# Four recurrent layers on one core: the first eight steps' PSUM banks begun one step at a time, the adapters' first products one step later, x of the first block loaded in two parts

## The chip, the cores and the metric

The kernel runs on one core of a Trainium2 chip. The metric is the time of one execution on the device in microseconds (us). Beside the times there is a profile of one execution, taken by the hardware profiler: when each instruction of each engine started and ended, and what it waited for. The engines are named PE (TensorE, matmuls; PEld are its weight loads), DVE (VectorE), ACT (ScalarE), POOL (GpSimd) and SP (SyncE, which issues the DMAs here).

## The reference

x is [32, 256, 256] (batch, time, features), cond is [32, 256]. Four layers follow each other, each added to x:

```python
# layer 0: GRU over time, conditioned          (h starts at 0)
z = sigmoid(x_t W_z + h U_z + cond C_z + b_z)
r = sigmoid(x_t W_r + h U_r + cond C_r + b_r)
hh = tanh(x_t W + r * h U + cond C + b)
h = (1 - z) * h + z * hh
# layer 1: leaky recurrence over time           (h starts at cond)
gate = sigmoid(h Wh' + x_t Wz' + b)
h = tanh(h * (1 - alpha) + gate * x_t)
# layer 2: gated cumulative sums over time, with W_f, W_i, W_h
# layer 3: adapter: matrices made from cond (W1, gelu, W2), applied to x per batch row
```

`r * h U` is `(r * h) @ U`. Everything is float32. Layers 0 and 1 are recurrences over 256 steps; layer 3's matrices depend on cond alone, and the gates of layer 2 for the first six eighths of the time can be computed while the recurrences still run.

## The kernel before, in words

**Two phases.** Phase 1 (lines 180 to 772) runs the two recurrences together, step by step: step t does layer 0 for time t and layer 1 for time s = t - 1. Phase 2 (lines 777 to 953) does what is left of layer 2, and layer 3, in ten turns over eight groups of four batch rows, by an order written out by hand (`TURN`). This change touches phase 1 only.

**The order.** Both phases stand under `tc.manual_schedule()`: each engine executes its instructions in the order of the program, and waits between engines are semaphores that the framework puts in. Work beside the recurrences is kept in dictionaries by step (`transfers`, `products`, `moves`, `additions`, `sigmoids`, `sums`, line 221), filled before the loop with `at(when, t, f)`, and called at fixed places of the loop with `due(when, t)`.

**One step on TensorE** (loop at line 693). In the order of the program: the product `hT` x `U_rz` (in texts: U_rz(t)), on which r and z depend; what `products` holds for this step; in step 1 the begin of layer 1's bank; the product for layer 1 with `w_l_Wz` (l_Wz); the product `rhT` x `U_h`, on which the candidate hh depends; `h1T` x `w_l_Wh` (l_Wh); then `project(t + 1)`, the product of the next step's x with `W_rzh` (W_x). Each product is 8 matmuls (2 halves of the contraction by 4 column strips of the array, line 571), and each float32 matmul shows as 2 weight loads and 2 matmuls in the profile, 16 in all. All of these are line 573. Between U_rz and U_h, ACT computes r (L657), DVE r * h (L725) and its transpose rhT (L649). Between U_h and the next U_rz, ACT computes tanh (L657), DVE a scan that combines z, h and hh (L639) and the transpose hT (L649).

**Banks and their begin.** The sums of a step are gathered in a PSUM bank of 512 columns: r, z and hh of one step take 3 x 64 = 192 columns, so a bank holds two steps, t and t + 2 (U0 = 2), and there are two such banks at a time. `begin` (line 593) writes the terms that do not depend on time (bias and cond's products, in `v`) with four matmuls, `start=True`, for all steps of the bank at once. For t < 8 it multiplies float32 `v` by an identity; from t = 8 on bfloat16 `parts`, prepared by DVE in steps 1 to 6 (lines 380 to 388: `rest` L237, `cast` L233). `project` calls it when a bank is new: for steps 0, 1, 4, 5, 8, 9 and so on, ahead of W_x of that step and thus at the end of the step before. Layer 1 has a bank of its own, for 2 steps first and then for 8 (`begin_1`, line 671); the first one of 8 steps is begun at the end of step 2, behind W_x(3), with float32 `v` and 512 columns.

**The adapters' weights** (`ada_weights`, line 400): eight pieces of W2. Piece n has its two products (`multiply`, L429, tile `pw`, here pw(0) and pw(1)) in steps t and t + 1, its four loads of 256 KB in transfers of steps t - 5 to t - 2, its bias at t - 2, a copy by ACT at t + 2, additions by POOL at t + 2 and t + 3, its store at t + 4. The first t is 5 (line 519), each next one 4 later. The adapters' matrices (`ada_matrix`, L489 and following) come after them, each in 6 steps. Layer 2's early gate products (`gate_unit`, L93 or L115) go into the steps from 35 on that have none of these (lines 535 to 557); phase 2 reads them back from DRAM.

**Loads at the start.** SP issues them in this order: cond, condT, vecs, bias rows, C_rzh (2), W1, x of steps 0 to 7 (`load_x(0)`, 256 KB), W_rzh (768 KB), U_rz (512 KB), U_h, l1_Wz, l1_Wh, x of steps 8 to 15, base_down, base_up (256 KB each).

## Time and profile before

| What | us |
|---|---|
| median of 3 runs | 955.35 |
| lowest and highest of them | 955.17, 957.66 |
| the profiled execution: its own time | 956.46 |
| the profiled execution: span from first to last instruction | 954.6 |
| phase 1 (until the first product of phase 2) | 737.6 |
| hT of step 0 begins | 13.96 |
| mean step over the recurrence | 2.82 |
| median step | 2.80 |

The granted TensorE clock was 0.995 of full speed. A step is counted from one hT (the first of the two transposes, L649) to the next. A row of the profile's timeline gives start, length, engine, line, operation, what is written and read, shape and count; in square brackets, how long the engine was idle before it and what ended that. "issue" there means that the profile shows nothing that the engine waited for. A row of the chain of waits gives start, length and engine, line and count of the work that was on the way to the end. Lengths of matmuls are those of a pipeline and overlap: the start of the next row tells what one cost.

### The profile page before, as it was taken

What the parts mean: (1) busy time and instruction counts of PE and PEld (TensorE: products, weight loads), DVE (VectorE), ACT (ScalarE), POOL (GpSimd) and SP (SyncE); (2) the same over time, 40 slices, a digit from 0 to 9 for tenths busy, and PEclk for the clock granted to TensorE, in tenths of its full rate; (3) what the DMA queues carried; (4) which work ended last, traced back from release to release, by engine and by line L of the source; (5) the groups of instructions that cost most, each with busy time, mean ns of one, the idle gap of its engine ahead of it and who ended that gap; (6) DMA issues with size and microseconds to landing.
All of it is one profiled execution on the core that took longest, in us unless ns stands there. A gap on an engine that the chain in (4) does not pass through costs nothing.

```text
span 954.6 us, 55121 instructions
## 1 busy us (share of the span) xinstructions
PE 919.4 (96%) x22806; PEld 630.6 (66%) x22806; DVE 788.4 (83%) x3409; ACT 572.3 (60%) x2648; POOL 236.5 (25%) x594
## 2 busy tenths in 40 slices
PE   7999999999999999999999999999998989999978
PEld 4666666666666666666666666666675557777756
DVE  5767788888888888888888888888776799999994
ACT  3455555555555555555555555555554788889972
POOL 1233322222222222222222222222222022222222
PEclk9999999999999999999999999999999999999989
DMA  8344212222222222222222222432241457777543
GB/s 265 108 126 147 79 51 92 65 73 92 70 92 77 92 66 67 91 70 90 69 86 76 65 97 66 131 119 83 73 128 54 122 165 230 224 228 224 188 158 117
DMA packets 104158, 107.71 MB, mean 113 GB/s; under 512 B 9153, under 2 KB 86241, under 8 KB 103906
## 3 DMA queue, kind: packets, MB, share of 16 engines
q1 hardware_dynamic: 103906, 104.18, 34.4%
q8 instruction: 179, 2.93, 1.3%
q14 instruction: 73, 0.60, 0.2%
HBM read 59.06 MB, written 45.09 MB: 109 GB/s over the span
## 4 chain that ended last, share of the span: by engine, by line
PE 80%; DVE 13%; ACT 3%; issue 2%; DMA 1%; POOL 0%; DVEq 0%; POOLq 0%; ACTq 0%
PE p L573 45%; PE ps_l L889 10%; PE pg L93 10%; PE ps_c L93 5%; DVE h L639 5%; PE p L600 3%; PE ps_g L93 2%; PE pw L489 2%; ACT other L657 2%; DVE hT L649 1%; ACT r L657 1%; DVE rh L725 1%; DVE cc L848 1%; DVE gate_g L138 1%; PE pw L429 1%
## 5 line engine op out<-in xcount | busy, mean ns | idle before, releaser
L573 PE MATMUL p<-w_W_rzh,xT 128*32 128x192 f32 x4096 | 214.8, 326 | 0.2 <-issue 0.2
L657 ACT ACTIVATE other<-p 128x32 f32<-128x32 f32 x512 | 74.2, 199 | 172.9 <-PE p L573 172.9
L639 DVE TENSOR_TENSOR_SCAN h<-other,keep 128x64 f32<-128x64 f32 x512 | 121.3, 278 | 66.3 <-ACT other L657 62.7
L573 PE MATMUL p<-w_U_rz,hT 128*32 128x128 f32 x4080 | 165.4, 279 | 6.0 <-DVE hT L649 0.2
L750 POOL TENSOR_TENSOR pairs<-xT,hT 128x64 f32<-128x64 f32 x256 | 82.2, 321 | 326.9 <-DVE other L766 273.6
L657 ACT ACTIVATE r<-p 128x32 f32<-128x32 f32 x510 | 72.8, 195 | 149.0 <-PE p L573 149.0
L689 POOL TENSOR_TENSOR X<-pairs,h1T 128x64 f32<-128x64 f32 x256 | 103.0, 402 | 214.9 <-DVE rhT L649 211.8
L573 PEld LDWEIGHTS p<-w_U_rz,hT 128*32 128x32 f32 x4080 | 97.4, 108 | 84.3 <-DVE hT L649 83.4
L639 DVE TENSOR_TENSOR_SCAN pre<-other,pairs 128x128 f32<-128x128 f32 x256 | 123.3, 481 | 34.2 <-ACT pairs L757 0.7
L573 PEld LDWEIGHTS p<-w_W_rzh,xT 128*32 128x32 f32 x4096 | 124.9, 110 | 22.4 <-issue 1.9
L573 PEld LDWEIGHTS p<-w_l_Wz,pairs 128*32 128x32 f32 x4096 | 79.2, 110 | 86.0 <-issue 69.2
L757 ACT ACTIVATE pairs<-h1T,leak 128x32 f32<-128x32 f32 x510 | 133.6, 314 | 0.4
L573 PE MATMUL p<-w_l_Wz,pairs 128*32 128x64 f32 x4096 | 120.3, 225 | 5.1 <-ACT keep L707 1.6
L573 PE MATMUL p<-w_U_h,rhT 128*32 128x64 f32 x4080 | 106.6, 221 | 0.4 <-issue 0.4
L573 PE MATMUL p<-w_l_Wh,h1T 128*32 128x64 f32 x4080 | 104.7, 219 | 0.8 <-issue 0.7
L725 DVE TENSOR_TENSOR rh<-r,h 128x32 f32<-128x32 f32 x510 | 74.9, 188 | 32.1 <-ACT r L657 5.7
L649 DVE STREAM_TRANSPOSE hT<-h 128x32 f32<-128x32 f32 x512 | 84.1, 198 | 0.0
L882 POOL TENSOR_TENSOR X<-X,w 128x512 f32<-128x512 f32 x32 | 41.4, 1306 | 165.3 <-DVE w L875 76.8
L649 DVE STREAM_TRANSPOSE rhT<-rh 128x32 f32<-128x32 f32 x510 | 80.0, 195 | 0.0
L573 PEld LDWEIGHTS p<-w_l_Wh,h1T 128*32 128x32 f32 x4080 | 76.4, 110 | 1.3 <-issue 1.0
L573 PEld LDWEIGHTS p<-w_U_h,rhT 128*32 128x32 f32 x4080 | 69.7, 108 | 5.5 <-issue 0.6
L686 ACT ACTIVATE h1T<-pre 128x64 f32<-128x64 f32 x256 | 69.5, 271 | 1.4 <-DVE pre L639 1.4
(108 smaller groups left out, 1470.5 us busy)
## 6 DMA issues: line engine op xcount, KB each, us to landing
adapted<-wm SPq DMA_DIRECT2D x128, 128.0 KB
wt<-adapted SPq DMA_DIRECT2D x28, 512.0 KB
xT<-in_xT_dram SPq DMA_DIRECT2D x32, 256.0 KB
w<-in_W_dram SPq DMA_DIRECT2D x32, 256.0 KB
out_dram<-y SPq DMA_DIRECT2D x32, 256.0 KB
gates<-gate_i SPq DMA_DIRECT2D x48, 128.0 KB
gates<-gate_s SPq DMA_DIRECT2D x48, 128.0 KB
gates<-gate_g SPq DMA_DIRECT2D x48, 128.0 KB
```

The lines of the kernel that those rows point to most:

```text
L93: nc.tensor.matmul(ps[:, 0 : (h1 - h0) * (rows.stop - rows.start) * CT].rearrange("p (h b t) -> p h b t", h=h1 - h0, t=CT), w[:, k, e * P ...
L573: last = nc.tensor.matmul(ps[j * B : (j + 1) * B, cols], hT[:, k, :], w[:, k, j, :], start=False, stop=False, skip_group_check=True, tile_ ...
L639: nc.vector.tensor_tensor_scan(*(x[:, ns].rearrange("p n u -> p (n u)") for x in (done, other, pairs)), 0.0, ALU.mult, ALU.add,)
L649: nc.vector.transpose(dst[:, c], src[:, bass.ts(c, B)])
L657: nc.scalar.activation(dst[:, bass.ts(c, B)], src[:, bass.ts(c, B)], function)
L686: nc.scalar.activation(flat(h1T), pre, AF.Tanh)
L689: return nc.gpsimd.tensor_add(X2[:, :, :, s], by_chunk(pairs1.pop(s)[:, :, 0]), h1s.pop(s))
L725: rh_done = nc.vector.tensor_mul(rh[:, cs], r[:, cs], h[:, cs])
L750: nc.gpsimd.tensor_add(by_chunk(pairs1[t][:, :, 0]), x_of(t), hT)
L757: nc.scalar.activation(by_chunk(pairs1[s][:, :, 1])[:, c], h1T[:, c], AF.Copy, scale=leak[:, c : c + 1],)
L882: after(nc.gpsimd.tensor_add(x, x, ws[g][:, b]), on_vector)
L889: nc.tensor.matmul(ps[:, e, :], matrices[row][:, m, k, e * P : (e + 1) * P], src[:, k, :], start=(k == 0), stop=(k == NC - 1),)
```

## The change

Three edits.

1. `begin` no longer makes its bank; `bank` does. For t < 8, `project` begins the 192 columns of its own step alone, in each step; from step 8 on the two steps of a bank are begun together, as before. The begin of layer 1's banks is the same as before.
2. The first piece of the adapters' weights has t = 6 instead of 5. All pieces, the adapters' matrices and what fills the steps between them follow from that t.
3. x of steps 0 to 7 is loaded in two DMAs: steps 0 and 1 where the whole was, ahead of W_rzh; steps 2 to 7 behind U_h.

```diff
         def load_x(i):
             xTs[i] = xp.tile([P, NC, TB, B], FP, name=f"xT_{i}", tag="xT")
-            nc.sync.dma_start(out=xTs[i], in_=a["xT"][:, i])
+            if i > 0:
+                nc.sync.dma_start(out=xTs[i], in_=a["xT"][:, i])
+
+        def load_first_x(steps):
+            nc.sync.dma_start(out=xTs[0][:, :, steps], in_=a["xT"][:, 0, :, steps])
...
             load_x(0)
+            load_first_x(slice(0, 2))
             w_x = load_wq("W_rzh", 3)
             w_urz = load_wq("U_rz", 2)
             w_uh = load_wq("U_h", 1)
+            load_first_x(slice(2, TB))
             w_1z = load_wq("l1_Wz", 1)
...
-        t = 5
+        t = 6
         for n in range(NW):
             ada_weights(n, t)
             t += 4
...
-        def begin(tag, cols, steps, t):
+        def bank(tag):
+            bufs = 2 if tag == "0" else 1
+            return pa.tile([P, 512], FP, name=f"p_{tag}", tag=f"p_{tag}", bufs=bufs)
+
+        def begin(ps, u, cols, steps, t):
...
-            ps = pa.tile([P, 512], FP, name=f"p_{tag}", tag=f"p_{tag}", bufs=2 if tag == "0" else 1)
             for j in range(Q):
                 nc.tensor.matmul(
-                    ps[j * B : (j + 1) * B, 0 : steps * n].rearrange("p (u n) -> p u n", n=n),
+                    ps[j * B : (j + 1) * B, u * n : (u + steps) * n].rearrange(
+                        "p (u n) -> p u n", n=n
+                    ),
...
         def project(t):
             if t // 2 % U0 == 0:
-                ps = begin("0", slice(0, 3 * S), U0, t)
-                for u in range(U0):
-                    p_0[t + 2 * u] = ps
+                p_0[t] = p_0[t + 2] = bank("0")
+                if t >= 8:
+                    begin(p_0[t], 0, slice(0, 3 * S), U0, t)
+            if t < 8:
+
+                begin(p_0[t], t // 2 % U0, slice(0, 3 * S), 1, t)
             return product(p_0[t], cols_0(t, 0, 2), x_of(t), w_x)
 
         def begin_1(s, steps):
-            ps = begin("1", slice(3 * S, 4 * S), steps, s)
+            ps = bank("1")
+            begin(ps, 0, slice(3 * S, 4 * S), steps, s)
```

More of the change, by code (lines that the diff above doesn't have):

```diff
@@ L608, in begin @@
                 )
-            return ps
         def cols_0(t, first, last):
```

## The prediction, made before the changed kernel ran

> **What bounds the kernel now.** I read the page's head and its DMA part first, then the chain of waits of the first 16 us, then TensorE's timeline from 8 to 30 us, then the start times of the hT transposes (L649) over the whole recurrence.

> ```profile
> span 954.6 us, 55121 instructions
> ...
> PE 919.4 (96%) x22806; PEld 630.6 (66%) x22806; DVE 788.4 (83%) x3409; ACT 572.3 (60%) x2648; POOL 236.5 (25%) x594
> ...
> q8 instruction: 179, 2.93, 1.3%
> ```

> PE's 96% is not the limit. One step runs from one hT to the next, and in 237 of 255 steps that takes 2.80 us within 0.03, whatever extra products stand in the step: the recurrence is a chain PE, ACT, DVE, PE. The last line counts PE's instruction blocks: 179 packets, 2.93 MB, thus 16,384 bytes each. It matters below.

> The chain of the start:

> ```profile
> 11.38 0.46 ACT hyT L373 x2
> 11.85 1.28 ACT L374
> 13.15 0.23 ACT keep L707
> 13.38 0.18 ACT other L657 x2
> ...
> 14.20 0.69 PE p L573 x16
> ```

> Step 0 is held by ScalarE: gelu (L373), its table load (L374), then z (L707). PE is not in it.

> The rows in which the changed work stands (start, length; 16 matmuls are one product):

> ```profile
> 15.63 0.43 PE L573 MATMUL p<-w_U_h,rhT 128*32 128x64 f32 x16
> 15.88 0.41 PE L573 MATMUL p<-w_l_Wh,condT 128*32 128x64 f32 x16
> 16.10 0.83 PE L573 MATMUL p<-w_W_rzh,xT 128*32 128x192 f32 x16
> 17.05 0.64 PE L573 MATMUL p<-w_U_rz,hT 128*32 128x128 f32 x16
> ...
> 18.96 0.83 PE L573 MATMUL p<-w_W_rzh,xT 128*32 128x192 f32 x16
> 19.61 1.04 PE L600 MATMUL p<-v,ident 128*32 128x512 f32 x8
> 20.47 0.62 PE L573 MATMUL p<-w_U_rz,hT 128*32 128x128 f32 x16
> ...
> 22.35 0.85 PE L600 MATMUL p<-v,ident 128*32 128x384 f32 x8
> 22.99 0.86 PE L573 MATMUL p<-w_W_rzh,xT 128*32 128x192 f32 x16
> 23.64 0.65 PE L573 MATMUL p<-w_U_rz,hT 128*32 128x128 f32 x16
> ...
> 26.83 0.62 PE L573 MATMUL p<-w_U_rz,hT 128*32 128x128 f32 x16
> 27.27 0.38 PE L429 MATMUL pw<-w,hyT 128*32 128x256 f32 x1
> 27.91 0.42 PE L429 MATMUL pw<-w,hyT 128*32 128x256 f32 x4 [0.26 <-issue]
> ```

> From U_h to the next U_rz, PE has a window of 1.42 us (15.63 to 17.05) that h's way through ACT and DVE takes anyway. Lengths overlap, so costs are differences of starts: U_h 0.24, l_Wh 0.23, W_x 0.65 (22.99 to 23.64); together 1.11, cover 0.30. A begin of 384 columns costs 0.64 (22.35 to 22.99), of 512 columns 0.86 (19.61 to 20.47), so 192 columns cost 0.32.

> **The begins.** Before: two begins of 384 columns at steps 0 and 1 (behind ACT and hT, free) and two ahead of U_rz(4) and U_rz(5). After hT's start U_rz can begin 0.24 later (16.81, 17.05). hT(3) starts at 23.00, so U_rz(4) is 23.64 - 23.24 = 0.40 late; hT(4) at 26.27, so U_rz(5) is 26.83 - 26.51 = 0.32 late. After: 0.32 in every step.
> - Steps 0 and 1 begin less: 0. U_rz(1) waited for hT, PE idle 0.5 us before it.
> - Ahead of U_rz(2): 0.32 into a cover of 0.30: +0.02.
> - Ahead of U_rz(3): begin_1's 0.86 already overfills that window, nothing covers: +0.32.
> - Ahead of U_rz(4) and U_rz(5): 0.32 less each: -0.32, -0.32.
> - Ahead of U_rz(6) and U_rz(7): PE idle 0.22 and 0.37 there; DVE's casts (L237, L233) stretch the window: 0, at worst +0.10.

> Sum -0.30. Were 192 columns no cheaper than 384 (0.64 each), it would be 0.34 + 0.64 + 0 + 0 + 0.42 + 0.27 = +1.7 instead.

> **Products a step later.** pw(0) leaves step 5 (3.41 us from hT to hT) for step 6. Without its stop at 27.27 step 5 would take about 2.87 between U_rzs instead of 3.08: -0.21. In steps 6 and 7 pw takes 0.42 in the window after U_rz, where step 6 shows it costs nothing. SP only issues the weights' loads later; they are needed at 29.9 instead of 27.2. The chain of adapters' matrices ends at step 234 instead of 233, gate products fill to step 254 instead of 253, the last gate store goes from step 257's place to 258's. None is on the path: phase 2 starts at 737.58 on POOL's X (L689), and first fetches of gates follow it. In step 256 DVE has the room for one guard (0.55): idle 1.10 ahead of its transpose. 0, bounded by -0.1 and +0.6.

> **x in two parts.** Before, 256 KB lie ahead of W_rzh, which lands at 11.87 (SP's next issue waits for it). 192 KB less at 0.75 us per 256 KB (landings 13.25, 14.01, 14.77) bring it about 0.55 earlier, and U_rz and U_h too. Step 0's z waits for the table load until 13.15, W_x(0) ends at 12.6 already: 0. The rest of x passes l_Wz and l_Wh, which have the same bytes ahead as before but more packets: by the trace's DMA records a 2,048-byte packet takes 86 ns, 768 bytes 36, 128 bytes 13, 512 bytes 27. Old: 128 x 86 / 16 = 0.69 us. New: 256 x (20, an estimate between 13 and 27) and 256 x 36, over 16 engines: 0.90. So l_Wz lands 0.2 later, at about 15.0 instead of 14.8, for a use at 14.89 that has 0.35 us before U_h: +0.0 to +0.1. One more DMA puts base_up's issue behind W_rzh's landing (SP's ninth DMA waits for the first); behind it on SP stand x of steps 16 to 23 and the adapters' loads for step 6. None is wanted within 10 us: 0. [...]

> **What the sum hides: PE's instruction blocks.** PE stops eight times in the recurrence with "issue", no releaser: at 18.35, 27.91, 44.58, 69.73, 103.25, 708.94, 712.96, 717.53 (starts after the stop). I counted PE's instructions (load, matmul, semaphore) in the trace: every one stands 194 or 193 past a multiple of 256, a 16,384-byte block, and 1.3 to 1.5 us after the end of a q8 packet. A packet starts about 0.8 us after the boundary before it, takes 1.0, and is used 1.4 later: 3.2 of the 4.1 us that PE takes for a block. When DMA is full it starts late. The steps over 2.80 after step 7 are 11, 20, 32, 42, 57, 247, 249, 250, by 0.54, 0.57, 0.30, 0.26, 0.16, 0.67, 0.64, 0.55: 3.69 us, most of them such stops. [...]

> The change moves these boundaries: each additional begin is 16 instructions. By step 5 begins 2 and 3 add 32. The boundary that stopped PE inside pw(0) then falls after the first pair of U_rz(5), on the chain. The boundary before it is at 22.35 now, 22.39 then (l_Wh(3)), and 5.56 us passed from there to 27.91, because the next weights' loads (issued 20.1 to 22.7, as before) fill DMA. So U_rz(5), due at 26.53, would go on at 27.95. From there 1.42 and, with DVE's L237, 1.44: U_rz(6) at 30.80 instead of 29.91. The first three parts and this together give **+0.9**; without the stop -0.5. I take +0.9, the row's own delay.

> After step 8 boundaries are 64 instructions, about 1.04 us, earlier; the adapters' DMAs 2.80 later. The block after (4.15 on) meets them with 4.15 - 1.04 - 2.80 = 0.31 us in favour. Each late stop shorter by 0.31 gives -2.3 of 3.69; x, gate weights and matrices don't shift, so I take the half and less: **-1.0**. Bounds: -3.7 (all go) to +3.7 (as many again).

> Sum +0.9 - 1.0 = -0.1. In the profiled execution (956.46, span 954.6, 1.86 outside) that is 956.4; it stands 1.1 above the median of the runs, 955.35, so I put the forecast at **955.2**.

> **Rivals.**
> 1. The stop at U_rz(5) doesn't come (its packet starts earlier), and late stops shrink as worked out: -0.5 - 1.0 to -2.3, at **953.6**. For it: W_x(0) and (1) run 0.6 earlier, so the first block is asked for earlier. Against: 22.35 is hardly moved. Chance 0.2.
> 2. Slower: boundaries fall onto U_rz or U_h instead of covered places. One stop costs up to 1.4 there (U_rz(5) above), against 0.2 in pw(0). With the +0.9 and one or two more late stops than now, **957.2**; four more decide for over 958.2. For it: packets 18 and 35 are used at 1.46 and 1.54 us after their end, just at the limit. Chance 0.2.
> 3. The begins are not hidden: PE pays 0.32 in all six steps, 1.92 - 0.72 saved = +1.2, with the stop 957.5. Against: PE idles 0.30 before 17.05. Chance 0.1.

> The forecast's case (954.2 to 956.3) has 0.5. About 0.3% (2.9 us) is what a measurement of this kernel can tell from no change, and the three runs of before span 2.5. Below 952.5 only rival 1's tail, 0.06; above 958.2 tails of 2 and 3, 0.08. The range 953.0 to 957.4 leaves out about 0.2.

> **What would show it.** hT(0) at 13.96 as before; U_rz(2) at 17.07; U_rz(3) 0.3 later, at 20.8; U_rz(4) at 23.66; an "issue" stop of about 1.4 in U_rz(5) at 26.5; steps 8 and on 2.80; stops 1.3 to 1.5 us after q8 packets, 64 instructions earlier. Wrong if step 0 gets shorter, if U_rz(2) starts over 0.2 later, or if a wait other than "issue" appears after step 8.

## The result, and the profile after

Over 14 executions of each kernel the changed kernel took 959.87 us (median; 957.28 to 962.21), the one before 957.09 (955.17 to 958.94): ratio 1.0028, 95% interval 1.0018 to 1.0039. A second comparison (r1 below, 12 executions against 35) gave 961.38 against 959.72, ratio 1.0018 (1.0002 to 1.0034). The change makes the kernel slower, by 2.8 us in the first comparison and 1.7 in the second; forecast was -0.1. The 955.35 that the forecast started from was the median of three runs, 1.7 below that of 14: of the 4.7 us between 955.2 and 959.87, 1.7 lie in the starting point and 2.9 in the change (+2.8 instead of -0.1).

The profiled execution took 961.18 (granted clock 0.989 of full speed). The lines of its page that answer to those of before:

```profile
span 959.4 us, 55161 instructions
...
PE 923.6 (96%) x22826; PEld 635.1 (66%) x22826; DVE 788.4 (82%) x3409; ACT 573.5 (60%) x2648; POOL 236.6 (25%) x594
...
q8 instruction: 179, 2.93, 1.3%
```

The work is the same, and as many instruction packets: 179 of 16,384 bytes for PE's 45,875 recorded instructions (45,837 before), 256 to a packet. The start, first ScalarE's timeline, then TensorE's:

```profile
12.04 0.47 ACT L379 ACTIVATE hyT<-ph,vecs 128x32 f32<-128x32 f32 x2 [6.01 <-PE ph L371]
12.51 1.28 ACT L380 ACT_TABLE_LOAD   x1
13.80 0.23 ACT L721 ACTIVATE keep<-p 128x64 f32<-128x64 f32 x1
```

```profile
14.85 0.64 PE L579 MATMUL p<-w_U_rz,hT 128*32 128x128 f32 x16 [0.63 <-DVE hT L659]
...
15.98 0.43 PE L579 MATMUL p<-w_l_Wz,pairs 128*32 128x64 f32 x16 [0.26 <-DMA w_l_Wz<-in_l_Wz_dram]
...
17.78 0.62 PE L579 MATMUL p<-w_U_rz,hT 128*32 128x128 f32 x16
...
21.50 0.62 PE L579 MATMUL p<-w_U_rz,hT 128*32 128x128 f32 x16
...
24.35 0.62 PE L579 MATMUL p<-w_U_rz,hT 128*32 128x128 f32 x16
...
27.20 0.63 PE L579 MATMUL p<-w_U_rz,hT 128*32 128x128 f32 x16
```

All of step 0 is 0.65 later (z at 13.80 instead of 13.15). Take that off, and U_rz(2) to U_rz(5) start at 17.13, 20.85, 23.70 and 26.55, where the prediction has 17.07, 20.8, 23.66 and 26.5. The predicted stop in U_rz(5) is not in this execution.

Why step 0 is later: TensorE's rows for the same 16 matmuls, before and after.

```profile
7.19 1.48 PE L341 MATMUL pv<-w_c,condT 128*32 128x384 f32 x16
```

```profile
7.10 2.23 PE L347 MATMUL pv<-w_c,condT 128*32 128x384 f32 x16
```

They are untouched by the change. Over all traces hT(0) starts between 13.7 and 15.7 us: from 13.9 to 15.3 without any of the edits, from 13.7 to 15.2 with all of them. The 0.65 are within that spread, so I take them for chance. The clock rows show 1.00 in both, so they do not name the cause.

Three stretches add up to a profiled execution: up to hT(0), the recurrence to hT(255), and the rest. After against before: 14.61 and 13.96; 721.35 and 719.74; 223.43 and 220.91. The first eight steps took 23.72 instead of 24.24 us, as the begins and pw(0) had it; the steps after them, of 2.80 each, were late by 6.4 us in sum instead of 4.0 (here and below, what steps over 2.85 us have above 2.80); and phase 2 took 2.5 us more, of which the prediction has nothing.

**Phase 2.** The windows view (busy time of each engine, then granted clock), first of before, then of after:

```profile
737.50:741.00 3.50, 3.42 (x8) 2.80 (x9) 0.00 (x0) 0.00 (x0) 0.14 (x2) 0.51 0.66 186
768.00:772.00 4.00, 4.00 (x20) 3.49 (x19) 4.00 (x5) 3.94 (x7) 0.50 (x2) 1.00 0.92 247
```

```profile
739.00:743.00 4.00, 2.86 (x7) 2.32 (x8) 0.03 (x1) 0.26 (x1) 0.44 (x2) 0.51 0.42 123
770.00:774.00 4.00, 3.45 (x8) 2.82 (x9) 4.00 (x5) 3.95 (x5) 2.22 (x3) 0.50 0.42 121
```

Both are at half clock near 738 (and near 925, of which below); after is so again at 770, and TensorE's timeline there shows the price, 6.70 us for 16 matmuls that took 3.72:

```profile
766.83 3.72 PE L889 MATMUL ps_l<-X,wt 128*128 128x256 f32 x16 [2.85 <-POOL X L882]
```

```profile
770.55 6.70 PE L903 MATMUL ps_l<-X,wt 128*128 128x256 f32 x16 [2.85 <-POOL X L896]
```

The idle time ahead of them is the same 2.85 us. The traces' halved stretches last 3.41 or 6.83 us and start on a grid of 3.41 us: those of after, at 739.06, 769.78 and 930.21, are 9 and 47 times 3.413 apart, those of before, at 737.57 and 925.30, 55 times. On that grid PE idled for 2.08 us (61%) of the window that ended at 769.78, just before the clock fell; before, it idled for 1.95 (57%) of the one that ended at 768.29, and the clock stayed. That is no threshold: in runs told below the clock also fell behind windows with 46% (e1, 734.62 to 738.04), 50% (b2, 738.28 to 741.69) and 51% of it idle (e13, 105.20 to 108.61). So the window need not be idle as a whole; what decides besides the idle share is open.

What the second stretch costs can be read across the traces of the kernels whose idle time on PE behind the recurrence was left as it is. From hT(255) to the end it is 220.5 to 221.7 us in the six that do not have it, 223.4 to 223.7 in the four that have one of 6.83 us (after, r1, e8 and e11, the last being the kernel before with 64 instructions more), and 221.3 in e10, which has one of 3.41.

**Theories.** F: PE's instruction blocks. The change moves the boundaries and the transfers, and blocks arrive too late where they arrived in time. C: the clock; the change only shifts phase 2 on the grid, and the excess is the second halved window. B, within F: it takes a burst of transfers ahead of the packet. N: chance.

### The profile page after: what moved, and what is told of

Same layout as the page of the kernel before. It is cut to its first block, busy times and chain, and to the rows that moved or that the text cites. A ratio compares the mean times of both kernels' runs of the same rounds, so it can differ in the third digit from the quotient of the medians.

```text
span 959.4 us, 55161 instructions
## 1 busy us (share of the span) xinstructions
PE 923.6 (96%) x22826; PEld 635.1 (66%) x22826; DVE 788.4 (82%) x3409; ACT 573.5 (60%) x2648; POOL 236.6 (25%) x594
## 3 DMA queue, kind: packets, MB, share of 16 engines
q8 instruction: 179, 2.93, 1.3%
## 4 chain that ended last, share of the span: by engine, by line
PE 81%; DVE 11%; ACT 3%; issue 2%; DMA 1%; SPq 1%; POOL 0%; DVEq 0%; POOLq 0%; ACTq 0%
PE p L579 45%; PE ps_l L903 11%; PE pg L93 10%; PE ps_c L93 5%; DVE h L649 4%; PE p L609 3%; PE ps_g L93 3%; PE pw L495 2%; ACT other L667 1%; DVE hT L659 1%; ACT r L667 1%; DMA w_l_Wz<-in_l_Wz_dram 1%; DVE cc L862 1%; DVE rh L739 1%; PE pw L435 1%
## 5 line engine op out<-in xcount | busy, mean ns | idle before, releaser
L649 DVE TENSOR_TENSOR_SCAN h<-other,keep 128x64 f32<-128x64 f32 x512 | 121.3, 279 | 65.7 <-ACT other L667 62.2
L764 POOL TENSOR_TENSOR pairs<-xT,hT 128x64 f32<-128x64 f32 x256 | 82.5, 322 | 324.8 <-DVE other L780 270.5
L649 DVE TENSOR_TENSOR_SCAN pre<-other,pairs 128x128 f32<-128x128 f32 x256 | 123.6, 483 | 34.8 <-POOL pairs L764 1.0
L903 PE MATMUL ps_l<-X,wt 128*128 128x256 f32 x256 | 64.1, 408 | 8.2 <-POOL X L896 8.2
```

The source lines that it names most:

```text
L649: nc.vector.tensor_tensor_scan(*(x[:, ns].rearrange("p n u -> p (n u)") for x in (done, other, pairs)), 0.0, ALU.mult, ALU.add,)
L764: nc.gpsimd.tensor_add(by_chunk(pairs1[t][:, :, 0]), x_of(t), hT)
L903: nc.tensor.matmul(ps[:, e, :], matrices[row][:, m, k, e * P : (e + 1) * P], src[:, k, :], start=(k == 0), stop=(k == NC - 1),)
```

## Experiments: the edits one by one

e1 is edit 1 alone, e2 is edit 2 alone (`t = 5` becomes `t = 6`), e3 is edit 3 alone. e4 adds 192 instructions to the changed kernel:

```diff
+                if 8 <= t < 32:
+                    for _ in range(2):
+                        nc.tensor.matmul(
+                            p_0[t][0:B, 384:386], ident[:, 0:B], ident[:, 0:2],
+                            start=True, stop=True, skip_group_check=True,
+                            tile_position=(0, 0),
+                        )
```

e4's output is off by 0.041 (relative error); e10's, below, with matmuls of the same form behind the last use of a bank's sums, is not. From this I infer that in e4 `start=True` also restarts the sums of that strip of the bank, so that h of steps 8 to 31 lacks part of its terms; no run shows the sums themselves.

> Edit 1 alone: begins step by step, the adapters' first t stays 5, x in one part. Theory F (late instruction blocks): steps 3 and 4 together 0.3 to 0.7 shorter, step 2 to 3 0.3 longer; PE's block boundaries stand 64 instructions earlier than in the kernel before while no DMA moves, so the late steps of the recurrence are others than in the kernel before and their sum decides: 955 to 960 with the sum of late steps (over 2.80 after step 7) between 1 and 6 us. Rival W (the work of the begins itself): +2.8 us, found in steps 1 to 8. Rival C (half clock in phase 2): no difference in the recurrence, all of it after 735 us.

> Edit 2 alone: the adapters' first t is 6, begins and x as before. Theory F: PE's block boundaries stand as before, the adapters' DMAs come 2.8 us later, so again other late steps: 955 to 960, sum of late steps 1 to 6 us; the step of 3.41 at pw(0) gets shorter by 0.2 to 0.5. Rival S (the shifted schedule is worse by itself, at the end of the recurrence): +2.8 us, in steps 234 to 256.

> Edit 3 alone: x of the first block in two parts. Theory F: boundaries and DMAs after the start stand as before, so the late steps are those of the kernel before (11, 20, 32, 42, 57, 247, 249, 250) and the time is the same within 0.5 us. Rival X (the two parts delay l_Wz and the rest): +0.3 to +1 us, all of it in hT of steps 0 to 2.

> The changed kernel with 2 float32 matmuls of 2 columns in each of steps 8 to 31, 192 PE instructions more, written to columns of the bank that nothing reads. From step 32 on PE's block boundaries then stand as in the kernel before (64 + 192 = 256). Theory F: the long late steps 194, 212 and 224 of the changed kernel (1.16, 1.43, 0.82 over) go or change, other ones come; 956 to 958.5. Rival C (phase 2's clock): nothing changes, 959.9. Rival W or X (the start): nothing changes, 959.9.

Measured, as ratio to the kernel before: e1 1.0005 (0.9987 to 1.0022), e2 1.0015 (0.9999 to 1.0031), e3 0.9995 (0.9982 to 1.0007), e4 1.0039 (1.0023 to 1.0055). No edit alone can be told from no change. e1 came out in its expected 955 to 960 us, e2 0.5 above it, and e3 within 0.5 of the kernel before; but e3's late steps were not those of the first trace, as F expected: of the eight named, only 20, 32, 249 and 250 are late by over 0.25 there. e4's matmuls cost 0.08 us in each step, 1.9 in all, so its time says nothing on F; its trace does: 194, 212 and 224, late in the changed kernel by 1.16, 1.43 and 0.83, are on time, and 114, 243 and 245 are late (1.05, 0.96, 1.49).

## Experiments: where the blocks fall, and what is in front of them

r1 is the changed kernel once more. e8 has `t % TB == 4` in place of `t % TB == 0` for x's loads. e10 (after) and e11 (before) add tiny matmuls behind `project(t + 1)`, where PE waits:

```diff
+                    if 8 <= t < 104 and t % 8 == 6:
+                        for _ in range(4):
+                            nc.tensor.matmul(
+                                p_0[t][0:B, 384:386], ident[:, 0:B], ident[:, 0:2],
...
```

(e11: `t < 40`, thus 64 instructions instead of 192.) b2 is the kernel before once more.

> The changed kernel as it is, once more, beside the other three. Theory F (PE's instruction blocks set which steps are late: the change moves each block's boundary 64 instructions earlier): the three large late steps 194, 212 and 224 come again in the profiled execution, each by 0.3 to 1.5 us, and steps 247, 249, 250, which were late before the change, are not late; hT(8) lies 23.7 after hT(0). Theory C (the excess lies in phase 2, where the clock is halved twice): the granted clock is halved in 0.5 us windows near 738 and again near 770 in about half of the executions, which then have a mean clock of 0.989 and are about 2.5 us longer than the others. Theory N (chance alone): late steps lie elsewhere, no mean excess. The time by F and C: 1.5 to 4 us over the kernel before; by N within 1.

> The changed kernel with the loads of x moved from steps 0, 8, 16... to steps 4, 12, 20..., so that a step has not both a load of x and the stores of an adapter. Theory B (the late stops at steps 194, 212, 224 come from 128 KB adapter loads, gate loads and 256 KB of x issued together): these stops fall below 0.4 us each, and the time is 2 to 3 us below the changed kernel beside it. Theory F alone (the place of the boundary decides): the stops stay at 0.5 us or more in sum over 1.5, and the time is within 1 us of the changed kernel.

> The changed kernel with 192 more PE instructions that nothing reads (4 tiny matmuls in each of 12 steps, 14 to 102, behind the product of x, at a place where PE waits), which moves all later block boundaries by 192 instructions, so that with the change's own 64 they stand again as in the kernel before. Theory F: the late steps 194, 212, 224 are gone, and steps 243 to 250 are late instead by 1.5 to 3 us in sum; the first hundred steps show small stops at other places; the time goes back by 0.5 to 2 us if the number of late steps does. Theory B: 194, 212, 224 stay, since the loads lie in the same steps. The 48 matmuls cost less than 0.3 us in all (0.4 us window).

> The kernel before the change, once more, for a second trace of it. Theory F (the place of the block boundaries decides which steps are late): late steps lie at 247 to 250 again, none of 0.5 us or more at 194, 212 or 224; the late steps after step 7 come to 3.5 to 5 us in sum, against 6.0 to 8.7 in the four traces of the changed kernel and of versions of it with the same boundaries. Theory N (the sum differs from execution to execution without regard to the kernel): 5.5 to 8 us, so that the 4.0 of the first trace was the low end. Theory C: the clock is halved near 738 once and not again near 770.

> The kernel before the change with 64 more PE instructions that nothing reads (4 tiny matmuls in each of steps 14, 22, 30 and 38, in a window where PE waits), so that from step 38 on its block boundaries stand where the change puts them, and all else is as before. Theory F: the late steps move to 194, 212 and 224, 1.5 us or more in sum, hT(255) comes 1 to 3 us later and the time is 1 to 3 us above the kernel before. Rival S (the excess comes from what the change does to the first eight steps or to the adapters' loads): the late steps stay at 247 to 250 and the time is within 0.6 us of the kernel before.

Ratios: r1 1.0018 (1.0002 to 1.0034), e8 1.0026 (1.0005 to 1.0046), e10 1.0019 (1.0000 to 1.0038), e11 1.0009 (0.9992 to 1.0027). The times do not separate these: e10's did not come back and e11's did not rise by the 1 to 3 us that F expected. The late steps by place do. What one looks like in TensorE's timeline of the changed kernel (block boundary inside the begin, step 212):

```profile
609.37 0.33 PE L609 MATMUL p<-parts,eye 128*32 128x384 bf16 x2
610.92 0.34 PE L609 MATMUL p<-parts,eye 128*32 128x384 bf16 x2 [1.22 <-issue]
610.92 0.98 PE L579 MATMUL p<-w_W_rzh,xT 128*32 128x192 f32 x16
```

And what SP issued ahead of it:

```profile
603.75 0.79 SPq L514 DMA_DIRECT2D adapted<-wm  x2
604.60 0.44 SPq L174 DMA_DIRECT2D wt<-adapted  x1
605.08 0.93 SPq L514 DMA_DIRECT2D adapted<-wm  x2
606.11 0.44 SPq L143 DMA_DIRECT2D gates<-gate_g  x1
606.59 0.46 SPq L174 DMA_DIRECT2D wt<-adapted  x1
```

Four stores of 128 KB, a gate store, two loads of 256 KB. The block's boundary before this one was passed at 605.97; the packet of instructions runs from 608.57 to 609.52, not 0.8 us after the boundary but 2.6; it is used 1.4 later, at 610.92.

Time above 2.80 us per step, summed over steps 194 to 230, in the traces:

| boundaries | adapters' transfers | traces | us |
|---|---|---|---|
| as before | as before | before, b2, e12, e14, e17, e3 | 0.00, 2.05, 0.29, 0.46, 0.67, 0.54 |
| as after | as before | e1, e11 | 1.76, 1.41 |
| as before | as after | e2, e10, e4 | 1.55, 1.03, 0.45 |
| as after | as after | after, r1, e9, e15, e16, e18 | 3.53, 2.42, 2.25, 2.09, 2.94, 2.73 |

(e9 to e18 are told below.) The rows' means are 0.7, 1.6, 1.0 and 2.7: each shift alone adds part, both together the most, and single traces of different rows come close (b2's 2.05). Steps 212 and 224 are late in every trace of the last row, by 1.08 to 1.43 and 0.83 to 1.09, and in no other row are both late by over 0.6. The third, 194, is late in after, e16 and e18 alone, not in r1, e9 and e15, against r1's expectation.

Here F is borne out for two steps, and b2 shows its limit: late steps from 8 on came to 9.7 us in it, 4.0 in the first trace of the same kernel, so N holds for single steps elsewhere. b2 (962.41 in its one execution) also missed its expectation under F: it was late at 211, 224 and 225 too. Over all steps from 8 on the five traces of the kernel before (e12, e14, e17 with it) come to 6.2 us on average (4.0 to 9.7), the six of the last row to 8.0 (6.4 to 9.0). With this spread the 1.8 between the means has a standard error of about 1.1 and is not clear of chance; the 2.0 at steps 194 to 230 has one of 0.4. Stops at a block boundary make most of the late time: 6.0 of 6.4 us in the first trace of the changed kernel, 3.1 of 4.0 in that of the kernel before. e8's 212 and 224 stayed (0.89, 1.00): loads of x are not the burst.

## Experiments: the burst taken apart

e13 issues an adapter's stores one to a step (`done + 1 + j` for `done + 1 + j // 2`) and moves the loads of 256 KB; e19 moves these loads alone:

```diff
-            at(transfers, T - 48 + 2 * n, load_matrices, row, slice(m, m + 1))
+            quiet = (207, 213, 215, 220, 226, 227, 231, 232)
+            at(transfers, quiet[n], load_matrices, row, slice(m, m + 1))
```

Both carry a fill that the next section shows.

> The changed kernel with the busy matmuls, and with its transfers spread: an adapter's four stores of 128 KB go one to a step instead of two, and the eight loads of 256 KB of its matrices, which stand at steps 208 to 222 among these stores, go to steps 207, 215, 220, 221, 226, 227, 232 and 233, in which no adapter's store begins. Theory B (a stop needs both a boundary and a burst of transfers ahead of the block's packet): the stops at 212 and 224 fall below 0.4 us each, the late steps after step 7 come to 4 to 6 us in sum, hT(255) 2 us earlier than with the busy matmuls alone, the time 1.5 to 2.5 us below that version (ratio to the kernel before about 0.9965). Theory F alone (the boundary's place in the step decides, whatever the transfers): 212 and 224 stay at 0.8 us or more each, the ratio stays at 0.9988.

> The changed kernel with the same fill, and the eight loads of an adapter's matrix (256 KB each), which stand at every second step from 208 to 222, moved to steps 207, 213, 215, 220, 226, 227, 231 and 232, which have no other transfer; the stores stay. Theory B (212 and 224 are late because a block's packet waits there behind these loads, issued together with stores of 128 KB): the late steps at 194 to 230 fall from 2.0 to 2.9 us to under 1, and the time is 1 to 2 us below the changed kernel with the same fill. Rival: the stops only move to other steps, the sum of the late steps stays at 7 to 8.5 us and the time within 0.7 us.

Ratios: e13 0.9981 (0.9962 to 1.0000), beside 0.9988 for the same fill alone in another comparison; e19 0.9973 (0.9956 to 0.9991), beside 0.9979 in the same one. 212 and 224 are gone in both (0.25 and 0.00; 0.00 and 0.00). TensorE's timeline of e19 at the boundary that stopped the changed kernel in step 212:

```profile
612.08 0.41 PE L580 MATMUL p<-w_l_Wh,h1T 128*32 128x64 f32 x16
612.30 0.35 PE L610 MATMUL p<-parts,eye 128*32 128x384 bf16 x4
612.47 0.83 PE L580 MATMUL p<-w_W_rzh,xT 128*32 128x192 f32 x16
```

The boundary before it was passed at 608.91, and the packet runs from 609.29 to 610.82: it starts 0.4 us after that boundary instead of 2.6. So B holds for the cause of these two stops: the boundary stands where it stood, and only the loads have moved.

The time did not follow. e19's median is 0.2 us above e18's (resampled: 2.3 below to 1.2 above), so the hoped-for 1 to 2 us are not shown, and not excluded either. The trace says where they may have gone: e19 is the same program as e18 up to step 206, and has 6.4 us of late steps there (194 by 1.16 among them), where the six traces of the last row have 3.2 to 3.8. From step 207 on it has 2.5 us, they 2.8 to 5.6. The gain at the stops that were taken out is of the size of what one execution has by chance elsewhere. In e13 likewise 4.0 us stand at steps 24 and 33, ahead of its first moved store in step 47.

## Experiments: the clock taken out of both

The fill puts matmuls that nothing reads into PE's idle time: e9 (after) and e12 (before) at the end of the recurrence and ahead of the gap near 770,

```diff
+                    if t == T:
+                        busy(2)
...
+                if turn == 2 and word == "lf:0":
+                    ps = pp.tile([P, NC, T], FP, name="ps_l3", tag="ps_l3", bufs=4)
+                    for _ in range(3):
+                        nc.tensor.matmul(
...
```

and further ones meant for a 4.97 us gap near 925: eight in a wrong place, behind the gap and not in it (e14 before, e15 after, e16 after without edit 3), four in the right one (e17 before, e18 after). `busy(1)` stands ahead of the last l_Wz as well. The matmuls have 512 columns (two expectations say 256) and cost 0.88 us each.

> The changed kernel with matmuls that nothing reads put into PE's idle time at the end of the recurrence: 16 in front of and 32 behind the last product of layer 1 (step 256), and 3 of 256 columns ahead of the first products of ps_l in phase 2. Theory C (PE's idle time around 735 and 770 halves the clock for 3.4 or 6.8 us, and that costs 2 to 3 us): the halved windows at 738 and 770 are gone, hT(255) to the end falls from 221 to 223.4 to about 219, mean clock 0.995 in all executions, time 2 to 3 us below the changed kernel beside it. Theory F alone: the time is within 0.7 us of the changed kernel, whatever the clock.

> The kernel before the change with the idle time of PE filled as in the run with the busy matmuls: 16 ahead of and 32 behind the last product of layer 1, 3 of 256 columns ahead of the first products of ps_l. Theory C: hT(255) to the end takes 218.4, against 220.9 before, mean clock 0.996 or 0.998, and the time is 1.5 to 2.5 us below the kernel before (ratio 0.9975 to 0.9985). If the halved clock costs only where it comes twice: within 0.7 us of the kernel before.

> The kernel before the change with all of PE's long idle times after the recurrence filled: the matmuls of the run before with the busy matmuls, and 8 more of 512 columns (about 3.6 us) in the 4.97 us in which PE waits for X ahead of the last but one group's first ps_l, near 925 us. Theory C: the halved windows at 738 and at 925 are both gone, the 16 matmuls of ps_l behind that wait take 3.6 us instead of 6.5, hT(255) to the end takes 216 to 217 against 219.2 with the first fill and 220.8 with none, the time is 4 us below the kernel before (ratio 0.995 to 0.997). If PE is not the bound there: no less than 218.2, ratio 0.9975.

> The changed kernel with the same fill, so that the halved clock weighs the same in both. Theory C as the whole cause of the difference between the two kernels: the time is within 0.7 us of the kernel before with the same fill. Theory F (the boundaries of the change make more late steps): 1.5 to 3 us above it. The sum of the change's lasting parts by the traces (POOL's last X 0.30 later, hidden here by the fill at most in part; the first eight steps -0.28 without and +0.25 with the stop at U_rz(5)): between -0.3 and +0.6.

> The changed kernel with the same fill and with x loaded in one piece as before the change (the begins step by step and the products a step later stay). POOL has then one semaphore instruction less: its pause of 0.38 us, which with the split comes between the last wait and the last X add, is gone there, X follows hT(255) by 3.50 instead of 3.80. Theory P (that pause is the split's whole cost): 0.3 us below the changed kernel with the same fill, too little for the clock of a run to show, so that the trace decides. Rival S (the split also costs at the start): more than 0.8 us below.

> The kernel before the change with the first fill (as in the run of it with the busy matmuls) and, in place of the 8 matmuls that fell into a busy stretch and took 7.03 us there, 4 of 512 columns (3.5 us at 0.88 each) ahead of the ps_l products that wait 4.97 us for X, near 925 us. Theory C: no halved window near 925; those 16 matmuls take 3.6 us instead of 6.5; from there on TensorE sets the end (the misplaced 7.03 us cost about 6), so hT(255) to the end takes 216 to 217 instead of 219.2 and the ratio to the kernel before is 0.994 to 0.996. If X of the next group sets the end instead: 218.5 and 0.9975.

> The changed kernel with the same fill. Theory F (more late steps at 212 and 224, the stop at U_rz(5), POOL's last X): 1.5 to 3.5 us above the kernel before with the same fill, with the tail from hT(255) alike in both within 0.5 us, and 212 and 224 late by 1.5 us or more in sum. Theory C (only the clock differed): within 0.7 us of it.

| | ratio to before | hT(255) to the end |
|---|---|---|
| e9, after | 0.9988 (0.9970 to 1.0006) | 218.4 |
| e12, before | 0.9977 (0.9962 to 0.9992) | 219.2 |
| e14, before | 1.0041 (1.0027 to 1.0056) | 225.7 |
| e15, after | 1.0070 (1.0047 to 1.0093) | 224.3 |
| e16, after less edit 3 | 1.0073 (1.0050 to 1.0095) | 224.6 |
| e17, before | 0.9949 (0.9931 to 0.9966) | 218.0 |
| e18, after | 0.9979 (0.9961 to 0.9996) | 218.3 |

The times of e9, e12, e15, e17 and e18 came out within what one of their theories expected, or beyond it in the same direction (e9); the tails expected of e12 (218.4), and of e14 and e17 (216 to 217), were not reached.

C holds for the tail: with the gaps near 738 and 770 filled the clock never fell there, and e9's tail is 5 us shorter than after's. The windows view of e17 shows full clock at all three places,

```profile
737.00:741.00 4.00, 3.68 (x24) 2.40 (x17) 0.43 (x1) 0.84 (x4) 0.44 (x2) 1.00 0.30 83
766.00:772.00 6.00, 5.95 (x28) 5.23 (x29) 6.00 (x8) 5.92 (x8) 1.72 (x2) 1.00 0.74 200
925.00:932.00 7.00, 6.51 (x30) 5.73 (x31) 7.00 (x10) 5.22 (x7) 2.11 (x2) 1.00 0.70 228
```

and TensorE's timeline of e12, then of e17, what the last of them is worth:

```profile
929.25 6.49 PE L904 MATMUL ps_l<-X,wt 128*128 128x256 f32 x16 [4.97 <-POOL X L897]
```

```profile
920.36 3.60 PE L903 MATMUL ps_l<-X,w_W_f 128*128 128x512 f32 x8
925.49 3.72 PE L911 MATMUL ps_l<-X,wt 128*128 128x256 f32 x16 [1.54 <-POOL X L897]
```

The 2.8 us gained on these 16 matmuls come only in part to the end (219.2 to 218.0): PE waits for POOL's X again, 1.46 us at 934.13. e14's misplaced matmuls took 7.03 us and cost 6.0 (e12's ratio times the 958.9 us of the kernel before in that comparison is 956.7; e14 took 962.7): there PE does set the end.

C as the whole cause of the change's cost falls. With the clock at 1.00 in both, e18 takes 957.58 us and e17 954.70: 2.9 us, ratio 1.0030 (1.0018 to 1.0045, from resampling the 12 and 11 times). e15 against e14 is the same to within its error (2.5 us, 0.5 to 4.3, with five executions of e15: a sixth took 2219 us and is left out). e9 against e12, each by its ratio to the kernel before in another comparison, comes to 1.1 us (-1.2 to 3.3), which fits but shows nothing alone. In the traces the difference lies in the recurrence: between hT(8) and hT(255) e18 needs 700.4, e17 696.7, with tails alike to 0.24. These two executions differ by 5.0 us, more than the medians do, and 1.4 of it is hT(0). e17 is also the fastest version here, 5.0 us (3.3 to 6.6) or 0.5% below the kernel before; its tail accounts for 2.8 of that (220.8 to 218.0), and the rest is not explained.

e16 shows what edit 3 leaves. POOL's timeline at the end of the recurrence, before and after:

```profile
737.20 0.33 POOL L689 TENSOR_TENSOR X<-pairs,h1T 128x64 f32<-128x64 f32 x1 [1.67 <-ACT h1T L686]
```

```profile
739.76 0.33 POOL L703 TENSOR_TENSOR X<-pairs,h1T 128x64 f32<-128x64 f32 x1 [1.97 <-ACT h1T L700]
```

The split gives POOL one more semaphore instruction (1164 recorded, 1163 before), from a second wait for x (L764). In the changed kernel, from 198 us on, a pause of 0.38 us stands between a wait and X at every 128th of POOL's recorded instructions, seven times, the last at the X on which phase 2 waits (before, that X starts 0.09 after its wait, and the 128th instruction is the one behind it). X comes 3.80 us after hT(255) instead of 3.50 in the traces with the split (4.03 in e4 and e10); e16, without it, has 3.50. The times of e15 and e16 do not show it, as expected of 0.3 us, and neither do their tails (224.3 and 224.6). The cause of the pause was not tried.

## Why the prediction was wrong, step by step

- **Begins, -0.30: right.** Steps 2 to 5 grew or shrank by +0.04, +0.32, -0.34 and, without stops, -0.32 (2.86 against 3.18).
- **pw(0), -0.21: wrong, by 0.2.** Six other traces that have the old begins and pw(0) in step 5 (b2, e3, e11, e12, e14, e17) need 3.17 to 3.18 there, not 3.41, and e2, with pw(0) gone, 3.17. The row counted was a stop that comes by chance; pw itself cost nothing.
- **x in parts, +0.0 to +0.1: right at the start, with a term missing at the end.** In the profiled execution W_rzh landed at 12.36 instead of the 11.3 predicted (SP's next issue stands there), and l_Wz at 15.84, not 15.0, and PE waited for it; that was hidden (step 1 took 2.86, 2.85 before). Landings differ by execution: in seven of the eleven traces with the split SP's issue stands at 10.6 to 11.2, as predicted, and only in two, e4 and e10, does step 1 take longer, by 0.38. The 0.30 of POOL's X was missing: I followed SP's queue past the new DMA, and not the wait that its second part adds on POOL.
- **Stop at U_rz(5), +1.4: right place, size too large.** It is in 9 of the 12 traces with edit 1, by 0.2 to 0.9; r1's TensorE timeline has the largest:

```profile
27.59 0.53 PE L579 MATMUL p<-w_U_rz,hT 128*32 128x128 f32 x12 [0.64 <-issue]
```

  With the typical 0.5 the first eight steps take 24.2 us, as before (24.0): the change's own gain goes into the stop that it makes.
- **Late stops after step 7, -1.0: the step that failed.** It came out near +1.8 (6.2 to 8.0 us on average, with an error of 1.1; at steps 194 to 230 alone 0.7 to 2.7, which is clear). I set the shift of boundaries (1.04 us earlier) against the adapters' (2.80 later) and got 0.31 us in favour of every block; but the loads of the matrices at steps 208 to 222 stay where they are, and the stores moved onto them: of this meeting the stops at 212 and 224 come, about 2 us, as e19 shows. "x, gate weights and matrices don't shift" was in the text, as a reason to halve a gain, not to look for a new meeting. Also, one trace's 3.69 us was taken as the kernel's; b2 shows 9.7. Rival 2 had nearly the size ("one or two more late stops than now", 957.2, 1.9 above the median it started from), at a chance of 0.2, but from boundaries falling onto U_rz or U_h, and its sum had the +0.9 of the start in it; the stop of step 212 stands in a begin, and what it takes is the burst.
- **Clock: absent from the prediction.** A second halved window came in the profiled execution, 2.5 us. By mean clock (0.988 to 0.990) it came in 10 of 26 executions of the changed kernel (the first 14 and r1's 12) and in 17 of 144 of the kernel before, beside the experiments; in r1's comparison alone in 3 of 12 and 1 of 35. The counts lean to the change, and no run tests why it should. In the first comparison the seven executions of the changed kernel at 0.989 took 960.9 us on average, the other seven 958.4, so 1.2 of its 2.8 us go with the clock there. e17 against e18 shows that a cost is there without it.

Added up from the traces: first eight steps +0.1, late steps +1.8, POOL's X +0.3, together 2.2 of the 2.9 measured in e18 against e17 (1.7 to 4.3). This is a sum of means over traces that differ among themselves by more, and no version shows the cost taken back by taking out its cause: the stops at 212 and 224 have their cause shown, the whole of the 2 to 3 us has not. Which edit costs how much stays open: alone none of them is measurable, and at steps 194 to 230 the block boundaries (edit 1) and the adapters' transfers (edit 2) both have a part.

## What to carry to other kernels

A step removed from a tuned loop moves everything behind it that is placed by count (instruction blocks, here by 64 instructions) but not what is placed by a fixed step: lay both schedules side by side and look for new meetings of a block boundary with a burst of transfers. Do not take stalls without a releaser from one trace as the kernel's: two traces here differed by 5.7 us in them. Where a trace shows the clock halved behind idle time of PE on the way to the end (here behind 2.85 us near 770 in the changed kernel and 4.97 near 925 in e12), matmuls that nothing reads can pay (e17 is 0.5% faster, of which its tail shows 0.3%), but only in true gaps (e14's, outside one, cost 6.0 us). A cause that is shown at one place of a trace need not show in the time: here chance moved as much elsewhere.
